# A top-2 mixture-of-experts layer in a two-layer decoder: from all eight experts for every token to 15 gathered blocks of 128 rows per group

## The chip, the cores and the metric

The kernel runs on one core of a Trainium2 chip. The metric is the device time of one execution in microseconds (us), the median over runs. The engines are called as the profile calls them: PE (TensorE matmul) and PEld (its weight load), DVE (VectorE), ACT (ScalarE), POOL (GpSimd) and SP (SyncE, which here only issues DMAs).

## The reference

Activations are `(128, 64, 128)` float32: 128 sequences of 64 tokens, 128 features. Six blocks follow one another, each a residual addition on a layer norm; only the last one changes.

```python
def _L1_ffn_ref(x, gate_W, W1, b1, W2, b2):      # E = 8 experts, 128 -> 256 -> 128, TOP_K = 2
    x_flat = x.reshape(-1, d_in)
    gates = jax.nn.softmax(x_flat @ gate_W, axis=-1)
    tk_g, tk_i = jax.lax.top_k(gates, TOP_K)
    tk_g = tk_g / (jnp.sum(tk_g, axis=-1, keepdims=True) + 1e-08)
    cw = jnp.sum(jax.nn.one_hot(tk_i, E, dtype=x.dtype) * tk_g[..., None], axis=1)
    out = x_flat
    for e in range(E):
        h = jax.nn.relu(x_flat @ W1[e] + b1[e])
        out = out + cw[:, e:e + 1] * (h @ W2[e] + b2[e])
    return out.reshape(x.shape[:-1] + (d_out,))

x = x + _L0_attn_ref(_layernorm(x), ...)     # Mamba-2 block with an MLP
x = x + _L0_xattn_ref(_layernorm(x), ...)    # pointer attention
x = x + _L0_ffn_ref(_layernorm(x), ...)      # ternary feed-forward
x = x + _L1_attn_ref(_layernorm(x), ...)     # causal attention, twice
x = x + _L1_xattn_ref(_layernorm(x), ...)    # cross attention
x = x + _L1_ffn_ref(_layernorm(x), ...)      # the experts
```

`cw` holds two non-zero weights per token: six of the eight experts' results are multiplied by zero.

## The kernel before

**Groups and layers.** The 8192 tokens are cut into 16 groups of 512 (`GT`), each eight sequences, held as four chunks (`C`) of 128 rows. `way(g)` (L1593) takes one group through the ten entries of `LAYERS` (L189), from "prepare" to "experts". A group's activations stay in one of seven SBUF buffers called x (`BUFS`, L186); L1596 loads it and L1603 stores it, and the next group may be loaded into the buffer when the store has landed. Each layer is a token of its own: one group at a time is in it, and up to seven groups are on their way together.

**The order of the work.** It is not written out by hand. `Turns` (L85) is a planner that runs while the program is built. Each piece of work is a generator; `yield V, 0.3` asks for 0.3 us of an engine (V, A, G, T stand for DVE, ACT, POOL, PE), `yield "a"` asks for a buffer of that name (PSUM bank "a": four, "fT": six transposed tiles, "hid": two), `yield None, 2.5` lets time pass for a DMA, and a list starts pieces side by side. The planner serves the process that holds a PSUM bank first, else the oldest request. The order in which it calls the instructions is the fixed order of each engine's queue; DMAs go to SP's queue as they are called. An engine then runs its queue strictly in order, so an instruction that waits holds back all that stands behind it.

**The layer at the end of each group** is `group(g)` in `experts` (L1460 to L1582):

- `norming` (L314): mean and variance on DVE (L283, L284), the root on POOL (L276, L277), the centring on POOL (L312, four instructions per group), then `turning` (L299): four transposes on PE (L305) and one copy by ACT (L307) give `uT`, features by tokens. POOL adds u to the residual (L1471).
- `gating` (L1476): four small matmuls give the logits; a softmax and two rounds of max, compare and rank on DVE leave `cw` (L1519), 128 x 4 x 8. Four transposes of `cw` (L1527), a copy (L1531), four matmuls with the bias table `b2` (L1537) and an addition (L1540) bring in the experts' second bias.
- `expert(e)` (L1552), eight times: `hidden` (L1543) multiplies a 128 x 128 half of `w1` with all 512 tokens (L1547, recorded as L200, the helper `mm`) and ACT takes the relu (L1549); eight matmuls of 128 columns with the halves of `w2` (L1561) leave the result in a bank, and DVE multiplies it by `cw` and adds it to X, a chunk at a time (L1571).

All eight experts' weights lie in SBUF from the start: `w1`, `w2`, `b2` are loaded at L1450 to L1452 (by `load`, L267, so the DMA is recorded at L269).

Of the kernel before, what the change touches and what calls it, by code (L numbers as in the profile page):

```python
# [26 lines left out]
I32 = mybir.dt.int32  # L27
# [12 lines left out]
E = 8  # L40
EXP_LN = "natural_log_exp_and_others"
# [5 lines left out]
def _constants():  # L47
# [26 lines left out]
    put("iota", np.broadcast_to(np.arange(S), (P, S)))  # L74
# [98 lines left out]
def tile_decoder(ctx: ExitStack, tc: tile.TileContext, w: dict, const: bass.AP, out: bass.AP):  # L173
# [12 lines left out]
    BUFS = {"u": 2, "fT": 6, "qm": 3, "km": 4, "x": 7, "hid": 2, "stats": 7, "pT": 12, "inv": 2, "sel": 1, "r2": 2, "r2T": 2, "ctxT": 2, "xdt": 1}  # L186


    LAYERS = ("prepare", "project", "recur", "mlp", "pointers", "ternary", "first", "second", "cross", "experts")  # L189
# [109 lines left out]
    def turning(o, parts, by=ident):  # L299

        yield "a"
        pt = bank("a", by.dtype)
        yield T, 0.12 * len(parts)
        for c, part in enumerate(parts):
            T.transpose(pt[:, c * P : (c + 1) * P], part, by)  # L305
        yield A, ac(P * len(parts))
        A.copy(o, pt)  # L307
        turns.give("a")
# [407 lines left out]
    def pointers(mp):  # L716
# [56 lines left out]
        def group(g):  # L773
# [49 lines left out]
            def ones():  # L823
                for n in range(3):
# [3 lines left out]
                        k["iota"].unsqueeze(1).to_broadcast([P, C, S]),  # L828
# [619 lines left out]
    def experts(mp):  # L1448
        gw = load("gate_W", [P, E], w["L1_ffn_gate_W"], mp)
        w1 = load("moe_w1", [P, E, 256], w["L1_ffn_W1"].rearrange("e d h -> d e h"), mp)  # L1450
        w2 = load("moe_w2", [P, E, 2, P], w["L1_ffn_W2"].rearrange("e (b p) d -> p e b d", p=P), mp)
        b2 = load("moe_b2", [E, P], w["L1_ffn_b2"], mp)  # L1452
# [7 lines left out]
        def group(g):  # L1460
# [3 lines left out]
            u = us[0]  # L1464
            yield "fT"
            uT = wk([P, GT], "fT", bufs=BUFS["fT"])
            yield from turning(uT, [u[:, c, :] for c in range(C)])

# [5 lines left out]
            cw = sm([P, C, E], "cw")  # L1474

            def gating():  # L1476
                yield "a"
                pl = bank("a")
                yield T, 0.9
                for c in range(C):  # L1480
                    mm(pl[:, c * E : (c + 1) * E], uT[:, c * P : (c + 1) * P], gw)
                lg = pl[:, : C * E].rearrange("p (c e) -> p c e", e=E)
                gates = sm([P, C, E], "gates")
                m = sm([P, 3, C], "gm")
                yield V, 0.3
                V.tensor_reduce(m[:, 0], lg, AX.X, ALU.max)
                V.tensor_tensor(gates, lg, over(m[:, 0]), ALU.subtract)  # L1487
                turns.give("a")
                yield A, 0.2
                A.activation(gates, gates, AF.Exp)  # L1490
                yield V, 1.2
                V.tensor_reduce(m[:, 0], gates, AX.X, ALU.add)
                V.reciprocal(m[:, 0], m[:, 0])
                V.tensor_tensor(gates, gates, over(m[:, 0]), ALU.mult)

                one = sm([P, 2, C, E], "one")
                top = sm([P, C], "top")
                for n in range(2):
                    V.tensor_reduce(m[:, n], gates, AX.X, ALU.max)
                    V.tensor_tensor(one[:, n], gates, over(m[:, n]), ALU.is_equal)  # L1500
                    V.tensor_tensor(one[:, n], one[:, n], k["rank"].unsqueeze(1).to_broadcast([P, C, E]), ALU.mult)
                    V.tensor_reduce(top, one[:, n], AX.X, ALU.max)
                    V.tensor_tensor(one[:, n], one[:, n], over(top), ALU.is_equal)
                    if n == 0:
                        V.scalar_tensor_tensor(
                            gates.rearrange("p c e -> p (c e)"),
                            one[:, 0].rearrange("p c e -> p (c e)"),
                            -2.0,
                            gates.rearrange("p c e -> p (c e)"),
                            ALU.mult,  # L1510
                            ALU.add,
                        )
                        yield V, 1.6
                V.scalar_tensor_tensor(m[:, 2], m[:, 0], 1e-8, m[:, 1], ALU.add, ALU.add)
                V.reciprocal(m[:, 2], m[:, 2])
                for n in range(2):
                    V.tensor_tensor(m[:, n], m[:, n], m[:, 2], ALU.mult)
                    V.tensor_tensor(one[:, n], one[:, n], over(m[:, n]), ALU.mult)
                V.tensor_tensor(cw, one[:, 0], one[:, 1], ALU.add)  # L1519

            yield [added(), gating()]

            yield "a"
            pt = bank("a")
            yield T, 0.48
            for c in range(C):
                T.transpose(pt[:E, c * P : (c + 1) * P], cw[:, c, :], ident)  # L1527
            yield "hid"
            cT = wk([P, 2, GT], "hid", bufs=BUFS["hid"])[:E, 0, :]
            yield V, dv(512)  # L1530
            V.tensor_copy(cT, pt[:E, :])  # L1531
            turns.give("a")
            yield "a"
            pb = bank("a")
            yield T, 1.0
# [109 lines left out]
```

## Time and profile before

| What | us |
|---|---|
| median of 3 runs | 2240.68 (2238.79 to 2242.68) |
| the profiled execution, device time | 2244.18 |
| its span, first to last instruction | 2242.4 |
| PE busy | 1943.9 (87%) |
| PEld busy | 1371.6 (61%) |
| DVE busy | 1473.1 (66%) |
| ACT busy | 1159.9 (52%) |
| POOL busy | 1018.7 (45%) |
| mean granted PE clock | 0.918 |
| DMA traffic | 53.61 MB, 24 GB/s on average |

The span is the part of the device time that the profile covers. An engine is busy while an instruction of it runs; instructions that only issue a DMA, wait, or load a register are not counted. A matmul of float32 is recorded as two instructions, so 256 matmuls stand as x512. "busy" of a group counts overlapped instructions once, "mean" is the length of one; for a pipelined engine the first, divided by the count, is what one costs in a stream.

### The profile page before, as it was taken

To read this page: it belongs to the slowest core of one execution; us is meant where nothing else is said; L and a number is where in the kernel's file an instruction comes from. 1 tells how busy PE (TensorE), PEld (TensorE's weight loads), DVE (VectorE), ACT (ScalarE), POOL (GpSimd) and SP (SyncE) were. 2 spreads that over 40 slices of the span, in tenths; PEclk is the share of its full clock that TensorE was granted. 3 is DMA by queue.
4 is the path that set the end of the run, shared out by engine and by line. 5 is a ranking of instruction groups with operands and counts; after the bars stand their busy time and mean duration, and the time that the engine had idled before them with its cause. 6 is when DMAs were issued, how large, how long until landed. Compare 5 with 4: busy or idle time off the path is not lost.

```text
span 2242.4 us, 56838 instructions
## 1 busy us (share of the span) xinstructions
PE 1943.9 (87%) x23919; PEld 1371.6 (61%) x23920; DVE 1473.1 (66%) x3991; ACT 1159.9 (52%) x2133; POOL 1018.7 (45%) x1258
## 2 busy tenths in 40 slices
PE   3777789889998899988998988999889898989996
PEld 1455556566675576666666566666666666756764
DVE  4578786777668567676776775767658567464443
ACT  1445455556465564655554555555537456554542
POOL 2566755554265426372645463435254526151121
PEclk8587788999998998999998989999989999999988
DMA  5111010000010000100101001000001001000000
GB/s 162 39 36 31 27 37 2 23 16 12 26 32 25 20 6 11 34 18 30 31 12 34 14 29 33 13 11 23 20 11 44 9 6 30 2 15 7 11 1 10
DMA packets 73451, 53.61 MB, mean 24 GB/s; under 512 B 30086, under 2 KB 59756, under 8 KB 73196
## 3 DMA queue, kind: packets, MB, share of 16 engines
q1 hardware_dynamic: 73196, 49.99, 7.4%
q8 instruction: 188, 3.08, 0.6%
q14 instruction: 67, 0.55, 0.1%
HBM read 41.45 MB, written 8.52 MB: 22 GB/s over the span
## 4 chain that ended last, share of the span: by engine, by line
PE 52%; DVE 27%; POOL 8%; ACT 8%; issue 3%; DMA 2%; SPq 1%; POOLq 0%; DVEq 0%; ACTq 0%
PE psa L200 36%; PE pss L200 11%; POOL u L312 4%; PE psa L305 4%; DVE tops L1202 3%; DVE x L1571 2%; DVE pT L1145 1%; DVE st L283 1%; DVE mv L284 1%; DVE amx L1157 1%; DVE pT L521 1%; DVE sel L855 1%; DVE s L861 1%; DVE h L1011 1%; DMA x<-in_x 1%
## 5 line engine op out<-in xcount | busy, mean ns | idle before, releaser
L312 POOL TENSOR_SCALAR u<-x,mv,rstd 128x128 f32<-128x128 f32 x320 | 259.6, 823 | 24.2 <-PE psa L305 13.4
L200 PE MATMUL psa<-fT,moe_w 128*128 128x512 f32 x512 | 257.8, 628 | 10.1 <-DVE pT L563 3.3
L200 PEld LDWEIGHTS psa<-moe_w,hid 128*128 128x128 f32 x2048 | 239.9, 192 | 27.6 <-issue 16.2
L1549 ACT ACTIVATE hid<-psa,vcol 128x512 f32<-128x512 f32 x256 | 174.6, 689 | 154.1 <-PE psa L200 151.1
L200 PE MATMUL psa<-moe_w,hid 128*128 128x128 f32 x2048 | 250.2, 277 | 3.0 <-DVE x L1571 1.4
L1571 DVE SCALAR_TENSOR_TENSOR x<-psa,cw,x 128x128 f32<-128x128 f32 x512 | 143.2, 343 | 154.3 <-PE psa L200 154.1
L276 POOL TENSOR_SCALAR rsq<-mv 128x4 f32<-128x4 f32 x96 | 23.4, 244 | 455.4 <-DVE mv L284 391.4
L1235 ACT ACTIVATE pT<-pss 128x512 f32<-128x512 f32 x256 | 146.2, 604 | 132.2 <-PE pss L200 131.9
L1159 POOL TENSOR_TENSOR pT<-pT,amx 128x512 f32<-128x512 f32 x128 | 132.8, 1061 | 110.2 <-DVE amx L1157 97.0
L1202 DVE TENSOR_REDUCE tops<-pss 128x32 f32<-128x2048 f32 x64 | 146.2, 2285 | 39.5 <-PE pss L200 39.3
L1034 POOL TENSOR_SCALAR r<-h 128x512 bf16<-128x512 f32 x64 | 97.2, 1526 | 126.7 <-DVE h L1032 83.4
L200 PEld LDWEIGHTS psa<-fT,moe_w 128*128 128x128 f32 x512 | 91.0, 197 | 92.4 <-issue 59.2
L200 PEld LDWEIGHTS pss<-km,qm 32*128 32x128 f32 x3072 | 101.8, 199 | 43.4 <-issue 34.0
L305 PE MATMUL psa<-cst,u 128*128 128x128 f32 x448 | 84.8, 306 | 45.9 <-POOL u L312 33.8
L200 PE MATMUL pss<-km,qm 32*128 32x128 f32 x3072 | 120.9, 297 | 0.1
L904 POOL TENSOR_TENSOR sel<-hot,s 128x256 f32<-128x256 f32 x64 | 44.3, 711 | 168.2 <-DVE s L898 138.9
L200 PE MATMUL psa<-pT,cst 128*32 128x256 f32 x1536 | 113.6, 405 | 6.0 <-DVE gates L1487 1.4
L617 POOL TENSOR_TENSOR qm<-qm,km 128x256 f32<-128x256 f32 x64 | 47.3, 740 | 155.3 <-DVE qm L612 153.8
L307 ACT COPY fT<-psa 128x512 f32<-128x512 f32 x112 | 65.5, 589 | 100.7 <-PE psa L305 99.7
L1275 ACT ACTIVATE inv<-psa 128x256 f32<-128x256 f32 x96 | 36.7, 383 | 139.0 <-PE psa L200 138.8
L1279 DVE TENSOR_TENSOR fT<-psa,inv 128x256 f32<-128x256 f32 x96 | 40.3, 420 | 99.9 <-ACT inv L1277 99.5
L305 PEld LDWEIGHTS psa<-cst,u 128*128 128x128 f32 x448 | 56.5, 152 | 73.1 <-POOL u L312 45.1
(284 smaller groups left out, 4698.4 us busy)
## 6 DMA issues: line engine op xcount, KB each, us to landing
pT<-steps SPq DMA_DIRECT2D x64, 256.0 KB, 3.9
x<-in_x SPq DMA_DIRECT2D x16, 256.0 KB
mask<-in_mask_Bx1xSxS_ff SPq DMA_DIRECT2D x32, 128.0 KB, 2.8
u<-in_ctx SPq DMA_DIRECT2D x16, 256.0 KB, 2.8
contexts<-ctxT SPq DMA_DIRECT2D x16, 256.0 KB, 2.0
ctxT<-contexts SPq DMA_DIRECT2D x16, 256.0 KB, 3.2
out<-x SPq DMA_DIRECT2D x16, 256.0 KB, 2.3
idg<-in_itok_BxS SPq DMA_DIRECT2D x32, 64.0 KB, 2.9
```

What stands on the lines that cost most here:

```text
L200: T.matmul(o, lhsT=lhsT, rhs=rhs, start=start, stop=stop)
L305: T.transpose(pt[:, c * P : (c + 1) * P], part, by)
L307: A.copy(o, pt)
L312: G.tensor_scalar(u[:, c, :], X[:, c, :], mean(c), scale[:, c : c + 1], ALU.subtract, ALU.mult)
L617: G.tensor_tensor(xc[:, :, cols], xc[:, :, cols], zs[:, :, cols], ALU.mult)
L904: engine.tensor_tensor(part[:, :, i, :], hot[:, n], s3[:, n, i, :].unsqueeze(2).to_broadcast([P, C, S]), ALU.mult,)
L1034: G.tensor_scalar(r2, h[:, c, :], -MAGIC, None, ALU.add)
L1159: G.tensor_tensor(s3, s3, mx.unsqueeze(2).to_broadcast([P, 8, S]), ALU.subtract)
L1202: V.tensor_reduce(mx[:, :, 0:8], banks.rearrange("p r (n s) -> p r n s", s=S), AX.X, ALU.max)
L1235: A.activation(pTs[r].rearrange("p b g q -> p (b g q)"), banks[:, r, :], AF.Exp)
L1549: A.activation(hid[:, b, :], ph, AF.Relu, bias=vec["moe_b1"][:, 2 * e + b : 2 * e + b + 1])
L1571: V.scalar_tensor_tensor(X[:, c, :], po_[:, c * P : (c + 1) * P], cw[:, c, e : e + 1], X[:, c, :], ALU.mult, ALU.add,)
```

## The change

Each token is sent to its two experts only. Per group the 1024 pairs (token, expert) are sorted by expert, each expert's list is padded to whole blocks of 128 rows, and there are at most (1024 + 8 x 127) // 128 = 15 blocks (`BLOCKS`), which are all computed.

- **Layers.** "experts" becomes three: "routing", "experts", "combine". The number of x buffers stays seven. New buffers: xg 2 (gathered rows of four blocks), we 3 (one block's weights), hg 2, yg 2.
- **Routing** (`routed`, `gating`, `routing`): norm and transpose as before; the 512 normed rows are also stored to DRAM (`urows`, two of them, used in turn). `gating` ends at the two one-hot rows and the two weights. `routing` finds each pair's place: two matmuls count the pairs before a row, DVE works out each expert's first block, and eight matmuls against one-hot tiles (`lanes`, 128 x 1024, and `tags`, 128 x 120) turn "which row goes to place p" into `of`, a list of row numbers by place. `to` holds the places by token, `expert` the expert of each block.
- **Experts** (`group`, `four`, `block`): POOL gathers the rows of a block from `urows` with an indirect DMA, one per block; four blocks are transposed together. SP reads the block's expert number from SBUF into a register and loads that expert's weights and both biases, 128 x 642 float32, from `packed`, a DRAM copy made at the start. Two matmuls of 128 columns, two relus by ACT, two matmuls, and a DVE addition of the bias finish a block, and each four blocks are stored to DRAM (`yrows`, two, used in turn).
- **Combine** (`combine`): POOL gathers each token's two result rows, two indirect DMAs per chunk, and DVE multiplies and adds them to X.

Removed are `cw`'s transposes and the bias matmuls, `hidden`, `expert`, and the SBUF copies of the weights. In `turning` the copy covers only the parts transposed.

```diff
+BLOCKS = (2 * GT + E * (P - 1)) // P
-    put("iota", np.broadcast_to(np.arange(S), (P, S)))
+    put("iota", np.broadcast_to(np.arange(P), (P, P)))
+    put("token", np.arange(C) * P + p[:, None])
+    put("before", p[:, None] < p[None, :])
...
-        A.copy(o, pt)
+        A.copy(o, pt[:, : P * len(parts)])
...
-        w1 = load("moe_w1", [P, E, 256], w["L1_ffn_W1"].rearrange("e d h -> d e h"), mp)
-        w2 = load("moe_w2", [P, E, 2, P], w["L1_ffn_W2"].rearrange("e (b p) d -> p e b d", p=P), mp)
-        b2 = load("moe_b2", [E, P], w["L1_ffn_b2"], mp)
+        WIDE = 256 + 2 * P + 2 + P
+        packed = dram.tile([E * P, WIDE], F32, tag="packed", name="packed")
...
+        urows = [dram.tile([GT, P], F32, tag=f"urows{i}", name=f"urows{i}") for i in range(2)]
+        yrows = [dram.tile([BLOCKS * P, P], F32, tag=f"yrows{i}", name=f"yrows{i}") for i in range(2)]
...
+        def whole(x):
+            V.tensor_scalar(x, x, MAGIC, None, ALU.add)
+            V.tensor_scalar(x, x, -MAGIC, None, ALU.add)
...
+        def routing(one, to, of, expert):
+            both = sm([P, C, E], "both", 1)
+            V.tensor_tensor(both, one[:, 0], one[:, 1], ALU.add)
...
+            yield T, 0.4
+            mm(pr[:, 0 : C * E], k["before"], bf)
+            mm(pr[:, C * E : 2 * C * E], k["ones"], bf)
...
+            V.memset(cum[:, 0], 0.0)
+            for c in range(C):
+                V.tensor_tensor(cum[:, c + 1], cum[:, c], total[:, c], ALU.add)
+            V.tensor_scalar(nb[:, 0], cum[:, C], (P - 1) / 2.0, 1.0 / P, ALU.add, ALU.mult)
+            whole(nb[:, 0])
+            V.tensor_tensor_scan(nb[:, 1], k["ones"][:, 0:E], nb[:, 0], 0.0, ALU.mult, ALU.add)
...
+            for n in range(2):
+                V.tensor_tensor(one[:, n], one[:, n], row, ALU.mult)
+                V.tensor_reduce(at[:, :, n], one[:, n], AX.X, ALU.add)
+            V.tensor_copy(to, at)
...
+            V.tensor_copy(expert, which)
+            yield "hid"
+            lanes = wk([P, 2, GT], "hid", bufs=BUFS["hid"]).rearrange("p n (l m) -> p (n l) m", m=P)
...
+            for i in range(2 * C):
+                mm(pi[:, 0:BLOCKS], lanes[:, i, :], tags[:, i, :], i == 0, i == 2 * C - 1)
...
+            V.tensor_copy(of, pi[:, 0:BLOCKS])
+        def routed(g):
             yield from norming(X, us)
+            rows, results = urows[g % 2], yrows[g % 2]
+            nc.sync.dma_start(rows.rearrange("(c p) d -> p c d", p=P), u)
             yield from turning(uT, [u[:, c, :] for c in range(C)])
...
+            yield [added(), gating(g, uT, one, m)]
+            turns.give("fT")
+            yield from routing(one, to, of, expert)
+        def group(g):
+            def four(first):
+                n = min(4, BLOCKS - first)
+                yield "xg"
+                xg = wk([P, 4, P], "xg", bufs=BUFS["xg"])
+                for i in range(n):
+                    yield G, 1.2
+                    G.indirect_dma_start(
+                        xg[:, i, :], None, rows, bass.IndirectOffsetOnAxis(of[:, first + i : first + i + 1], 0)
+                    )
+                yield None, 2.5
...
+                yield from turning(xT[:, 0 : n * P], [xg[:, i, :] for i in range(n)])
+                yield [block(first + i, xT[:, i * P : (i + 1) * P], xg[:, i, :]) for i in range(n)]
...
+                nc.sync.dma_start(
+                    results[first * P : (first + n) * P, :].rearrange("(i p) d -> p i d", p=P), xg[:, 0:n, :]
+                )
+            def block(i, xT, y):
+                yield "we"
+                we = wk([P, WIDE], "we", bufs=BUFS["we"])
+                e = nc.values_load(
+                    expert[0:1, i : i + 1],
+                    engines=[nc.sync.engine],
...
+                nc.sync.dma_start(we, packed[bass.ds(e * P, P), :])
+                yield None, 3.5
...
+                for b in range(2):
+                    mm(ph[:, b * P : (b + 1) * P], we[:, b * P : (b + 1) * P], xT)
...
+                    A.activation(
+                        hg[:, b, :], ph[:, b * P : (b + 1) * P], AF.Relu, bias=we[:, 2 * 256 + b : 2 * 256 + b + 1]
+                    )
...
+                for b in range(2):
+                    mm(py[:, 0:P], hg[:, b, :], we[:, 256 + b * P : 256 + (b + 1) * P], b == 0, b == 1)
...
+                V.tensor_tensor(y, py[:, 0:P], we[:, 514:WIDE], ALU.add)
+            yield [four(first) for first in range(0, BLOCKS, 4)]
+        def combine(g):
+            def chunk(c):
+                yield "yg"
...
+                for n in range(2):
+                    yield G, 1.2
+                    G.indirect_dma_start(
+                        yg[:, n, :], None, results, bass.IndirectOffsetOnAxis(to[:, c, n : n + 1], 0)
+                    )
+                yield None, 2.5
+                for n in range(2):
...
+                    V.scalar_tensor_tensor(
+                        X[:, c, :], yg[:, n, :], m[:, n, c : c + 1], X[:, c, :], ALU.mult, ALU.add
+                    )
+            yield None, 2.5
+            yield [chunk(c) for c in range(C)]
+        stages["routing"], stages["experts"], stages["combine"] = routed, group, combine
```

## The prediction

> **What bounds it now.** First the page's busy times and its 40 slices, then the stretches of the steady part, then SP's DMAs in order of time.
>
> ```profile
> PE 1943.9 (87%) x23919; PEld 1371.6 (61%) x23920; DVE 1473.1 (66%) x3991; ACT 1159.9 (52%) x2133; POOL 1018.7 (45%) x1258
> ...
> PEclk8587788999998998999998989999989999999988
> ...
> PE 52%; DVE 27%; POOL 8%; ACT 8%; issue 3%; DMA 2%; SPq 1%; POOLq 0%; DVEq 0%; ACTq 0%
> ```
> ```profile
> 600.00:900.00 300.00, 272.65 (x3879) 194.78 (x3879) 205.53 (x551) 164.02 (x310) 142.41 (x179) 0.94 0.06 18
> ...
> sum 1500.00, PE 1345.79 PEld 954.33 DVE 1034.53 ACT 823.17 POOL 725.95; mean PE 269.16 PEld 190.87 DVE 206.91 ACT 164.63 POOL 145.19
> ```
> ```profile
> 658.85 0.40 SPq L1603 DMA_DIRECT2D out<-x  x1
> 661.17 0.39 SPq L1596 DMA_DIRECT2D x<-in_x  x1
> ...
> 1628.19 0.39 SPq L1603 DMA_DIRECT2D out<-x  x1
> 1630.52 0.38 SPq L1596 DMA_DIRECT2D x<-in_x  x1
> ```
>
> From 300 to 1800 us PE is busy for 1345.8 of 1500 us (90%), DVE 69%, POOL 48%: PE is the bound there. But the time is also a chain of three stays in an x buffer. Every later x load stands 2.3 us behind a store. The second group enters at the start and leaves at 659; the ninth takes its buffer and leaves at 1628; the sixteenth takes that one and ends the span at 2242. **So what lengthens one group's way is paid three times, what is taken from PE comes back only as far as PE is on that chain.** Of the chain that ended last PE holds 52% x 2242 = 1166 us, 60% of its busy 1944; DVE 605 of 1473, 41%; POOL 179 of 1019, 18%.
>
> **PE, per group.**
>
> ```profile
> L200 PE MATMUL psa<-fT,moe_w 128*128 128x512 f32 x512 | 257.8, 628 | 10.1 <-DVE pT L563 3.3
> L200 PE MATMUL psa<-moe_w,hid 128*128 128x128 f32 x2048 | 250.2, 277 | 3.0 <-DVE x L1571 1.4
> ```
>
> Removed: (257.8 + 250.2) / 16 = 31.75 us, bias matmuls 20.7 / 16 = 1.3, `cw`'s transposes 10.7 / 16 = 0.7: 33.7. Added: 15 blocks of four matmuls, two records each, at 250.2 / 2048 = 0.122 us (the same shape): 14.65; 15 transposes at 71.3 / 512 = 0.14 (the row pT of L305): 2.1; the ten routing matmuls, 20 records at the same 0.122: 2.4. Sum 19.2, so **-14.5 us per group**, -232 in all.
>
> A rule speaks against this step. The Trainium skill, "TensorE: Matmul & The Clock Gate", Back-to-back issue gap, gives a sustained 81 ns for 128 columns and 131 ns for 512: a narrow matmul costs 62% of a wide one. By it the 30 narrow hidden matmuls would cost 18.5 wide ones where 16 stood, 2.5 us more per group. The rows say 0.122 against 0.503 us, 24%: 7.3 us for 16.1. I take the rows, which are this kernel's float32. By the rule the step would save 14.5 - 8.8 - 2.5 = 3.2 us per group, and the sum below would end 88 us later.
>
> **DVE, per group.** Removed: 32 x 143.2 / 512 = 8.95, L1531 and L1540 0.68 each, four small ones of `gating`: 11.1. Added: 15 bias additions and 8 combining ones at 0.28: 6.4; routing: 31 small ones at 0.19 to 0.22 (the last group's gating runs one each 0.22 us), `lanes` of 1024 columns about 1.25 (L826: 458 ns for 256), `tags` and `past` 0.3 each: 8. So **+3.4 us**.
>
> **ACT, per group.** Out 174.6 / 16 = 10.9; in 30 relus of 128 columns at 0.31 (row junk<-u, same width) and four copies at 0.59: 11.6. Nothing, since ACT is half idle.
>
> **POOL, per group: 15 + 8 indirect DMAs.** No row shows one. Below stands SP's issue of a DMA, 0.39; above, the 2.9 us in which the 64 KB load idg<-in_itok lands, if POOL were held all that time. Nearest is POOL's own fixed-cost instruction, L277, 1.04 us for 128 x 4. I take 1.2: 27.6 us on top of 1018.7 / 16 = 63.7, **91 us per group**, beside PE's 121.5 - 14.5 = 107 and DVE's 95. POOL is no bound by that, but no longer free: behind a gather in its queue stand the centrings (L312), whose transposes PE waits for, and the roots (L276) before them. The gathers also bring waits: one for a free xg buffer, that is for the store of earlier blocks to land, and combine's first for the last `yrows` store. If these come late, all of that stands still, for every group under way.
>
> The second rule that speaks against it: the Trainium skill, "SBUF — State Buffer", SBUF: two separate sides, on the "DVE blocks DMA" trap: a descriptor generation on GpSimd is shut out while DVE runs a two-port operation; 620 ns became 3100.
>
> ```profile
> L312 POOL TENSOR_SCALAR u<-x,mv,rstd x320: 782/792/2907, 133.9 to 2194.0; 128x128 f32<-128x128 f32 x160
> ```
>
> Here POOL's centring has a median of 792, a mean of 823 and a worst of 2907 ns: such waits occur, and cost 4% on average. By the row a gather is 1.25 us, by the rule up to 1.2 + 2.5 = 3.7, and POOL 149 us per group. I take the row; the rule widens the top of the range.
>
> **DMA and SP.** 240 weight loads of 321 KB (79 MB), 368 gathers of 64 KB (24 MB): some 75 GB/s on average where the first slice shows 162, so bandwidth is not the limit. A weight load is taken at 4.3 us (pT<-steps, 256 KB, lands in 3.9). The register load before it is not in the trace: between an event's 0.017 and 2.9 us; it waits for nothing but `expert`, so it runs while the load ahead waits for its buffer, and costs the path nothing; at 2.9 SP would hold 43 us more per group, and steps, masks and x loads behind it would be late. Behind a weight load that waits for its buffer stand those same DMAs; the planner calls it when the buffer is given back, so I cost it nothing, and take the 3.3 us per block that a late one could bring (2.9 and an issue) as part of the range. `packed` is written once, in the first 100 us, and first read after 479, where the first group reaches L1471: nothing.
>
> **The longer way of one group,** from the last group, which is nearly alone. Its rounds of compare end at 2201.7, its last addition (L1571) at 2238.9. Changed: three more operations of gating 0.7, routing's DVE work 8.7, 20 matmul records at 0.235 (gating's 8 took 1.88 there, at a granted clock of 0.50) 4.7, hops 0.6: list ready at 2216.4. Four gathers 4.8, landing 2.4, transposes and copy 1.3: 2225. A weight buffer is held for 4.3 + 0.47 + 0.62 + 0.47 + 0.34 and four hops of 0.2 = 7 us; three of them give a block each 2.33 us, 15 blocks 35 us: 2260. Store 2.7, eight gathers 9.6, landing and two additions 3: 2275. **+36 us**, three times: +108.
>
> **Sum.** The other 13 groups on the chain's way: PE -14.5 x 13 x 60% = -113; POOL +27.6 x 13 x 18% = +65; DVE +3.4 x 13 x 41% = +18. With +108: **+78 us** on the profiled execution's 2244.2 (span 2242.4), so 2322; the median of the runs is 3.5 us below that: **2319 us**. One gain is in none of these terms: in before a group holds the last layer alone, from L1471 at 1081.7 to its store at 1182.0, and the next begins at 1195.1, so that layer is occupied almost without a break; in three stages two groups overlap. Worth between nothing (PE is full anyway) and the idle tenth of PE, 150 us over the steady part. I take nothing and leave it to the first rival.
>
> **Rivals.**
> 1. *PE's relief comes back whole* (faster). For it: PE at 90%, a ninth less work, and a last layer that is now split. Against: POOL, DVE and PE come within 16 us of each other, in strictly ordered queues, with still seven groups. If the longer way counts only at the end: -232 + 36 = -196, 2045; with PE's fill over the span falling from 87 to 82% it is 1712 / 0.82 = **2090**. It decides where a gather holds POOL for about 1 us or less.
> 2. *POOL becomes the bound.* A gather at 2.9 us makes 63.7 + 66.7 = 130 us per group, above PE's 107: in my sum +39.1 x 13 x 18% = +92, and on the three ways 3 x 23 x 1.7 = +117: **2525**. Against: the mean of L312.
> 3. *Cancels*: within 5 us of before, where way and relief are equal.
>
> That it does not do what it says is excluded: 15 blocks are computed whatever the routing.
>
> **Numbers.** 0.50 for 2319 (2245 to 2420), 0.29 for the first rival, 0.18 for the second, 0.03 for the third (0.2% is what a measurement can tell). Faster 0.29, same 0.03, slower 0.68. The range 2120 to 2500 leaves out the lower part of rival 1 and the upper of rival 2. With slower cases at 0.68, the likeliest's own range stands above.
>
> **What would show it.** PE's busy time near 1712 us (step 1); a gather's hold on POOL and POOL's waits for it; DVE near 1520; from the last compare to the last addition of the last group 73 us instead of 37; x loads still behind stores, with stays of over 967 us in the middle. Wrong if PE stays near 90% in the middle (rival 1), or if POOL's queue is full (rival 2).

## The result and the profile after

The changed kernel takes **2526.3 us**, median of 4 runs (2513.42 to 2537.8), against 2240.8 beside it (2238.79 to 2242.68): a ratio of 1.1266 (95% interval 1.1232 to 1.1301), 286 us slower. The forecast had the direction; its size, 78 us, was far too small, and 2526 lies beyond its range.

The page after, busy times and granted clock by slices:

```profile
PE 1918.6 (76%) x23648; PEld 1424.2 (56%) x23648; DVE 1566.9 (62%) x4279; ACT 1166.9 (46%) x2421; POOL 1381.7 (55%) x1626
...
PEclk8677899999979888999697899989788988896655
```

PE was to fall by 232 us and fell by 25. The mean granted clock went from 0.918 to 0.851: PE is idle more often, and the last slices stand at 5 to 6. POOL rose by 363, about the 367 that its 368 gathers are busy. The same stretches as before (columns: stretch, its length, then busy us and count for PE, PEld, DVE, ACT, POOL, then clock, DMA share, GB/s):

```profile
600.00:900.00 300.00, 250.02 (x3581) 187.06 (x3582) 195.00 (x530) 151.21 (x320) 167.78 (x194) 0.90 0.28 73
...
sum 1500.00, PE 1212.64 PEld 901.18 DVE 1010.78 ACT 761.00 POOL 869.78; mean PE 242.53 PEld 180.24 DVE 202.16 ACT 152.20 POOL 173.96
```

From 300 to 1800 us PE is now busy 81% of the time (before 90%), DVE 67%, POOL 58%. No engine is full, so something waits. SP's DMAs show where the groups leave:

```profile
848.44 0.40 SPq L1739 DMA_DIRECT2D out<-x  x1
...
850.81 0.38 SPq L1732 DMA_DIRECT2D x<-in_x  x1
...
1796.53 0.39 SPq L1739 DMA_DIRECT2D out<-x  x1
...
1798.90 0.40 SPq L1732 DMA_DIRECT2D x<-in_x  x1
...
2525.49 0.38 SPq L1739 DMA_DIRECT2D out<-x  x1
```

The chain of three stays is still there, but it did not lengthen evenly: the second group leaves 190 us later than before (848 against 659), the stay in the middle takes 946 us instead of 967, and the last one 727 instead of 608. The first group alone is 132 us late: it stores its rows for the gathers at 480, when before it entered the last layer at 479, and leaves at 691 instead of 559.

POOL's longest wait in total is for the store of earlier blocks out of the buffer that a gather fills (total us, times, longest):

```profile
POOL xg L1643 <- DMA yrows<-xg: 162.5, 19, 23.1
```

What a group does in between is shown for the ninth one. First POOL in order of time (start, length; in brackets the idle time before and what ended it), then PE:

```profile
1616.16 1.12 POOL L1643 DMA_INDIRECT xg<-urows,of  x1 [0.18 <-issue]
1623.69 0.94 POOL L1643 DMA_INDIRECT xg<-urows,of  x1 [6.42 <-DMA yrows<-xg]
...
1626.36 1.03 POOL L1705 DMA_INDIRECT yg<-yrows,to  x1 [0.17 <-issue]
1627.69 0.94 POOL L1705 DMA_INDIRECT yg<-yrows,to  x1 [0.30 <-issue]
1628.94 0.94 POOL L1643 DMA_INDIRECT xg<-urows,of  x1 [0.30 <-issue]
...
1636.49 3.25 POOL L316 TENSOR_SCALAR u<-x,mv,r 128x128 f32<-128x128 f32 x4
1639.90 1.03 POOL L1643 DMA_INDIRECT xg<-urows,of  x1 [0.17 <-issue]
1640.98 3.12 POOL L316 TENSOR_SCALAR u<-x,mv,rstd 128x128 f32<-128x128 f32 x4
...
1654.53 0.99 POOL L1643 DMA_INDIRECT xg<-urows,of  x1 [0.16 <-issue]
```
```profile
1651.96 0.66 PE L309 MATMUL psa<-cst,xg 128*128 128x128 f32 x4 [1.25 <-DMA xg<-urows,of]
1657.04 0.48 PE L309 MATMUL psa<-cst,xg 128*128 128x128 f32 x1 [4.42 <-DMA xg<-urows,of]
1657.31 3.06 PE L204 MATMUL psa<-fT,we 128*128 128x128 f32 x12
```

A gather holds POOL for 0.94 to 1.12 us, with 0.30 between two: the 1.2 of the forecast. But the eight that the two xg buffers can take spread from 1616.2 to 1655.5, 39 us. The second stands 6.42 us for the store out of the buffer's last tenant; the others come behind the combining gathers of the group ahead and the centrings and additions of other groups. Only at 1657 does PE meet the first of these blocks, having waited 4.42 us for the last row. The group ahead stored its last block at 1620.9, so for some 36 us no block is computed; from 1697 to 1720, 23 us, no block is computed either: the gathers of the second pair of fours spread from 1685 to 1711. One group at a time is in this layer, and the next group's first gather comes within 14 us, before or behind, of its last store, from the second group to the last: the layer is never empty, and yet in this stay of 135 us (1616 to 1751) it computes no block for 59.

### The profile page after: what moved, and what is told of

The parts are those of the page before. It is cut to its first block, busy times and chain, and to the rows that moved or that the text cites. A ratio compares the mean times of both kernels' runs of the same rounds, so it can differ in the third digit from the quotient of the medians.

```text
span 2529.0 us, 59384 instructions
## 1 busy us (share of the span) xinstructions
PE 1918.6 (76%) x23648; PEld 1424.2 (56%) x23648; DVE 1566.9 (62%) x4279; ACT 1166.9 (46%) x2421; POOL 1381.7 (55%) x1626
## 5 line engine op out<-in xcount | busy, mean ns | idle before, releaser
L1643 POOL DMA_INDIRECT xg<-urows,of x240 | 239.2, 997 | 366.0 <-DMA yrows<-xg 162.5
L1678 ACT ACTIVATE hg<-psa,we 128x128 f32<-128x128 f32 x480 | 156.1, 369 | 220.4 <-PE psa L204 187.4
L204 PE MATMUL psa<-fT,we 128*128 128x128 f32 x960 | 182.3, 335 | 71.6 <-DMA we<-packed 53.4
L311 ACT COPY fT<-psa 128x512 f32<-128x512 f32 (+1 forms) x176 | 101.4, 579 | 262.0 <-PE psa L309 249.6
L204 PEld LDWEIGHTS psa<-fT,we 128*128 128x128 f32 x960 | 153.8, 234 | 101.5 <-issue 39.3
L1689 DVE TENSOR_TENSOR xg<-psa,we 128x128 f32<-128x128 f32 x240 | 67.7, 287 | 205.7 <-PE psa L204 204.8
L204 PE MATMUL psa<-we,hg 128*128 128x128 f32 x960 | 173.8, 318 | 23.5 <-ACT hg L1678 5.3
L204 PEld LDWEIGHTS psa<-we,hg 128*128 128x128 f32 x960 | 145.3, 220 | 43.9 <-ACT hg L1678 12.2
L1705 POOL DMA_INDIRECT yg<-yrows,to x128 | 128.0, 1000 | 56.6 <-issue 28.2
L204 PE MATMUL psa<-pT,v_a 128*32 128x64 f32 x4096 | 87.8, 227 | 13.0 <-issue 12.6
```

What stands on the lines that cost most here:

```text
L204: T.matmul(o, lhsT=lhsT, rhs=rhs, start=start, stop=stop)
L311: A.copy(o, pt[:, : P * len(parts)])
L1643: G.indirect_dma_start(xg[:, i, :], None, rows, bass.IndirectOffsetOnAxis(of[:, first + i : first + i + 1], 0))
L1678: A.activation(hg[:, b, :], ph[:, b * P : (b + 1) * P], AF.Relu, bias=we[:, 2 * 256 + b : 2 * 256 + b + 1])
L1689: V.tensor_tensor(y, py[:, 0:P], we[:, 514:WIDE], ALU.add)
L1705: G.indirect_dma_start(yg[:, n, :], None, results, bass.IndirectOffsetOnAxis(to[:, c, n : n + 1], 0))
```

## Experiments

All times are medians against the kernel before on the same chip (2238 to 2241 us); e1 to e4 ran on chip 0, e5 to e8 on 13, e9 to e12 on 15, e13 to e16 on 3, e17 and e18 on 11. The theories' names (SP, POOL, LENGTH, STAGE, X and so on) are those of the expectations. "Stage pitch" is the time from the first group's last store of blocks to the last group's, divided by 15, read in SP's order: 124.1 us in the changed kernel; the kernel before has 112.0 from output to output.

**Kernels e1 to e4: loads, buffer, price, width.**

```diff
 e1                                           e2
-  e = nc.values_load(expert[0:1, i:i+1])     -  V.tensor_tensor(y, py[:, 0:P], ...)   # y = xg
-  nc.sync.dma_start(we, packed[e])           +  V.tensor_tensor(xT, py[:, 0:P], ...)  # xg given back
+  we = held   # expert 0, loaded once                                                 # after turning
 e3                                           e4 (kernel before)
+  yield None, 2.5                            -  mm(ph, w1[...], uT)
   turns.give("xg")                           +  four mm of 128 columns each
```

e2 and e3 also leave out the 2.5 us that the planner lets pass before `combine`; e2 lets them pass before the transposed rows are given back.

> Leaves out the choice of a block's weights: every block computes with expert 0's, loaded once, so the 240 register loads and 240 weight loads of SP are gone. The order of the instructions on every engine is that of the changed kernel. Theory SP (weight loads that wait for one of three buffers hold up SP's queue, and with it steps, masks, contexts, stores and x loads): most of the 286 us is won back, 2330 us or less, and PE no longer waits for a weight tile (53 us after). Theory POOL (gathers that wait for the store from their xg buffer hold up the roots and centrings behind them): at most 50 us are won, 2475 or more, and POOL's waits for the store of blocks stay near 160 us. Theory LENGTH (simply more steps in series for a group): between the two, since a block loses 4 us of landing but keeps all else; about 2450.

> A block's result is written over its slice of the transposed rows and stored from there, so an xg buffer is free once it is transposed, and no gather waits for a store. Theory POOL: the 162 us in which POOL stood before gathers are gone and 100 to 200 us are won, 2330 to 2430. Theory SP: POOL's waits fall, but the time stays within 40 us, 2485 to 2565. Theory LENGTH: the same, within 40 us.

> Only the planner's times change: the buffer of gathered rows counts as free 2.5 us after the store was issued instead of at once; instructions, buffers and what they wait for are those of the changed kernel, their order is new. Theory that the planner's missing price makes the POOL waits: POOL's waits before gathers fall from 162 us to under 60, and 60 to 150 us are won. Theories SP and LENGTH: within 40 us of 2526. If POOL's waits stay, it is drift between the planned and the real times, not this price.

> The kernel before, with each 512-column product of the hidden layer issued as four of 128 columns. It measures the width price that the prediction took from the rows. By the rows (0.122 against 0.503 us a record): PE's busy time and the time stay within 20 us of before, 2241. By the ratio of the rule that the prediction set aside (a narrow one costs 62% of a wide one): 32 wide products per group of 0.503 become 128 of 0.31, 24 us per group more, 380 us of PE, and some 230 us of time, 2470. Theory PE (blocks cost 0.19 us a record because they are narrow): the new records cost 0.19 us, PE's busy rises by 16 x 32 x 2 x 4 x 0.19 - 258 = 520 us or so.

Measured: e1 **2450.5** (ratio 1.0978, 1.0937 to 1.1018; pitch 118.9), e2 **2535.1** (1.1340, 1.1313 to 1.1366), e3 **2587.4** (1.1553, 1.1516 to 1.159), e4 **2242.6** (1.0017, 1.0005 to 1.003).

e1 falsifies theory SP in its strong form: with all 240 weight loads gone, 76 of the 286 us come back, and the time is the 2450 that LENGTH named. In the changed kernel SP stands 760 us before weight loads whose buffer is not free (total us, times, longest):

```profile
SPq L1667 <- DVE xg L1689: 760.3, 136, 48.6
```

So about a tenth of that wait is paid in time. e2 moved POOL's wait and did not remove it, and its time, 9 us longer, is where SP and LENGTH had it. POOL's waits in e2:

```profile
POOL yg L1707 <- DMA yrows<-fT: 238.5, 11, 41.3
POOL rsq L280 <- DVE mv L288: 189.4, 31, 27.6
```

No gather of rows waits for a store any more, but now combine's first gather of a group stands up to 41 us for the last blocks. POOL takes its instructions in the planned order; whichever of them depends on blocks that are behind plan stops it. e3 shows two things: the price alone did not cure the waits (135.7 us before gathers of rows, 100.6 before those of combine), and a new order with no instruction changed is worth +61 us here, more than any theory allowed. e4 settles the width: by the rule that the forecast set aside it would be some 230 us slower, and it is 3. The row of the hidden layer's products in 128 columns (busy us, mean ns):

```profile
L200 PE MATMUL psa<-fT,moe_w 128*128 128x128 f32 x2048 | 263.7, 283 | 10.3 <-DVE pT L563 3.3 <-ACT qm L1076 2.8 <-ACT hid L1550 1.4
```

263.7 us for four times the instructions of before's 257.8: 0.129 us a record. In this kernel's float32 a narrow product costs about what its columns cost (0.129 against 0.503). The products of the changed kernel's blocks cost more:

```profile
L204 PE MATMUL psa<-fT,we 128*128 128x128 f32 x960 | 182.3, 335 | 71.6 <-DMA we<-packed 53.4 <-DVE m L894 4.2 <-ACT hg L1678 2.5
L204 PE MATMUL psa<-we,hg 128*128 128x128 f32 x960 | 173.8, 318 | 23.5 <-ACT hg L1678 5.3 <-ACT r2T L311 3.3 <-issue 2.2
```

That is 0.19 and 0.18 us a record. They come four records at a time, 0.61 to 0.71 us a burst at the higher clock and 1.2 at the lower. Width is excluded by e4; that short bursts and the lower clock make the difference is what the rows suggest, not something that a run isolated.

**Kernels e5 to e8: the single stay.**

```diff
 e5: layer "experts" has two tokens instead of one, three pairs of DRAM tables
 e6:
-    for i in range(n):
-        yield G, 1.2
+    yield G, 1.2 * n
+    for i in range(n):
         G.indirect_dma_start(xg[:, i, :], None, rows, ...)
 e7: e2 and e6, and  turns.give("fT", 2.5)   # free 2.5 us later, the group is not held back
 e8: e7 and e5
```

> The planner lets two groups be in the experts layer at once (with three pairs of row tables in DRAM instead of two); buffers, instructions and everything else are those of the changed kernel. Theory STAGE: one group at a time is in the stage of gathers and blocks, it stays there 128 us on average, the next begins within some 5 us, so the time is 509 (first gather) + 16 x 128 + 18; by it, overlap of the stays must shorten the time, here by 3 to 10 us per group because both groups still share two xg buffers and three weight buffers: 2370 to 2480. Theory LENGTH (steps in series for one group, paid three times through the seven x buffers): nothing is taken from a group's way, within 30 us of 2526. Theory that PE or POOL is full: within 30 us too, or slower.

> POOL's gathers of four blocks are asked of the planner as one turn of 4.8 us instead of four turns of 1.2, each behind whatever POOL has been asked meanwhile. In the changed kernel the 8 gathers of two such turns spread over 39 us in one group (1616 to 1655) where they take 10 us of POOL, and no block computes meanwhile. Theory STAGE: a stay loses 10 to 20 us, 160 to 300 us in all, 2230 to 2370. Theory POOL (what stands behind the gathers is what is late): centrings and roots are later by up to 3.6 us each turn, no gain or slower, 2500 to 2600. Theory LENGTH: 10 to 20 us three times, 30 to 60 us, 2470 to 2500.

> One group at a time as in the changed kernel; results written over the transposed rows (an xg buffer is free once it is transposed), the planner counts a row buffer as free 2.5 us after the store was issued without holding the group back, and the gathers are asked for in one turn. Theory STAGE: the second pair of gathers no longer waits for the first pair's blocks, so a stay loses the second empty stretch (35 us in the group looked at) and some of the first: 25 to 45 us, and the time falls by 300 or more, 2000 to 2230 unless another bound takes over near 2150. Theory LENGTH: 25 to 45 us three times, 2390 to 2450. Theory POOL: as in the run with results over the rows alone, near 2530.

> All of the run before it, and two groups in the experts layer at once. Theory STAGE: the stay is no bound any more, the time is that of the engines: POOL 88 us and PE some 110 us per group, 2050 to 2200, faster than the kernel before. Theory LENGTH: no better than with one group, within 30 us of that run.

Measured: e5 **2441.7** (1.0898, 1.0871 to 1.0924; pitch 118.1), e6 **2487.1** (1.1110, 1.1067 to 1.1152; pitch 121.9), e7 **2410.5** (1.0753, 1.0722 to 1.0784), e8 **2408.7** (1.0739, 1.0702 to 1.0777; pitch 116.7). Letting two groups in wins 85 us with no SBUF buffer and no instruction changed, within the range that STAGE named. The other sizes that STAGE named were too large (e6 wins 39 of 160 to 300, e7 116 of 300 or more), and e6, e7 and e8 came out where LENGTH had them. In e7 the layer stands empty for up to 107 us ahead of a group, in e8 for up to 63, and their times hardly differ. So the single stay may have been one bound, of some 85 to 118 us, with another close beneath it. That is not shown: each of the four is also a new order.

**Kernels e9 to e12: x buffers, and loads again.** e9 is e1, e10 the kernel before, each with `"x": 8` (e10 makes room by one buffer instead of two for the small tiles `gates` and `one`); e11 is e8 with `"x": 8, "xg": 1`; e12 is e8 with e1's edit.

> The kernel of e1 (every block computes with expert 0's weights, held in SBUF; no register and weight loads, otherwise as changed) with eight x buffers instead of seven; the room is that of the two weight buffers that e1 no longer has. Against e1's 2450.5. Theory LENGTH, which is the prediction's (a chain of three stays in an x buffer): with eight buffers the sixteenth group has one group before it in its buffer instead of two, so one stay of the three goes, and 100 us or more are won, 2350 or less. Theory STAGE (the experts layer holds one group at a time and is never empty): an eighth group only waits longer before that layer, 2420 to 2480.

> The kernel before with eight x buffers (the room is made by one buffer each instead of two for the two small tiles gates and one). Before, the last layer is empty for 87 us ahead of the eighth group, which waits for the first group's x buffer, and for 55, 51 and 17 elsewhere. Theory X (that gap is the wait for the buffer): 40 to 90 us are won, 2150 to 2200. Theory that PE is full at 90%: within 25 us of 2240.

> The kernel of e8 (two groups in the experts layer, results over the transposed rows, gathers in one turn) with eight x buffers; the room is made by one buffer of gathered rows instead of two, which can only slow a stay. In e8 the stage stands empty for 63 us ahead of the eighth group and 20 to 60 us ahead of others, so it is no bound there. Theory X (with the stage relieved the x buffers bind again): 60 to 150 us are won against e8's 2409, 2260 to 2350. Theory ENGINES (PE at 82% and POOL at 60% in strict orders is all that can be had): within 40 us of 2409.

> The kernel of e8 without the register and weight loads (every block computes with expert 0's weights, held in SBUF). SP still stands 700 us in e8 before weight loads whose buffer isn't free, with the steps, masks and x loads behind them. Theory SP: once the stage is relieved these waits are what binds, 100 to 200 us are won, 2210 to 2310. Theory ENGINES or X: as in e1, the landings alone, 30 to 80 us, 2330 to 2380.

Measured: e9 **2417.2** (1.0770, 1.0735 to 1.0806), e10 **2252.4** (1.0045, 1.0031 to 1.0059), e11 **2349.0** (1.0469, 1.0446 to 1.0492; pitch 110.8), e12 **2325.7** (1.0368, 1.0342 to 1.0394; pitch 111.5). With an eighth buffer the kernel *before* is 12 us slower, where theory X named 40 to 90 us won. The order is new there and two small tiles lost a buffer, so this is weak evidence, but it gives no sign that the x buffers bind. The chain of three stays through seven buffers stays true as a description of who waits for whom. In e9 the eighth buffer wins 33 us, where LENGTH named 100 or more. e11 wins 60 against e8, the least that theory X named. The loads are worth 83 us in e12, much as in e1 and less than SP named.

**Kernels e13 and e17: the gathers themselves.**

```diff
 e13 = e1 and                                       e17 = e13 and, before each of these loads,
-  G.indirect_dma_start(xg[:, i, :], ...)           +  G.tensor_scalar(fill, fill, 1.0, None, ALU.mult)
+  nc.sync.dma_start(xg[:, i, :], rows[i*P:(i+1)*P])
   (the same for yg)
```

> The kernel of e1 without the sorting: instead of POOL's 23 gathers per group SP loads 64 KB of rows in their plain order (and every block computes with expert 0's weights); the order of everything else on PE, VectorE, ScalarE and POOL is that of the changed kernel. Against e1's 2450.5. Theory POOL GATHERS (the 39 us in which a stay waits for gathers spread over POOL's queue): the stay falls from 124 us to under 105, and the time by 150 to 300 us, 2150 to 2300. Theory ORDER (the planner's order on PE and POOL, which is unchanged, keeps the blocks where they are): within 60 us of e1, 2390 to 2450.

> The kernel of e13 (no gathers on POOL, plain loads by SP, expert 0's weights for every block) with an operation of 128 x 160 elements on a tile of its own, about 1 us, in the place of each of POOL's 368 gathers: POOL is as busy as with them, but these wait for nothing, and rows don't come through POOL. Against e13's 2245 and e1's 2450.5. Theory TIME (POOL's occupied time is the cost): 2390 to 2450. Theory WAITS (what the gathers wait for and hold up, and that rows come only at POOL's turn): 2245 to 2310.

Measured: e13 **2245.0** (1.0018, 1.0008 to 1.0028; pitch 106.4), e17 **2265.9** (1.0118, 1.0078 to 1.0159; pitch 107.8). With the order of all other work as in the changed kernel, 205 us go with the gathers; loads and gathers together are 281 of the 286. On the page of e13 POOL is back at its busy time of before, and the chain that ended last is mostly PE and DVE, as before:

```profile
PE 1804.3 (80%) x23647; PEld 1354.4 (60%) x23648; DVE 1522.5 (68%) x4279; ACT 1161.9 (52%) x2421; POOL 1019.8 (45%) x1258
...
PE 43%; DVE 31%; ACT 11%; POOL 6%; DMA 4%; issue 4%; SPq 1%; ACTq 0%; POOLq 0%; DVEq 0%
```

e17 gives POOL an occupation back in the gathers' places. It came out shorter than meant, 0.61 us instead of 1:

```profile
L1646 POOL TENSOR_SCALAR fill<-fill x240: 597/609/1554, 506.4 to 2211.2; 128x160 f32<-128x160 f32 x120
L1700 POOL TENSOR_SCALAR fill<-fill x128: 598/608/1177, 641.8 to 2216.7; 128x160 f32<-128x160 f32 x128
```

POOL's busy time rises by 226 us to 1246, and the time by 21. Scaled to the gathers' 367 busy and their pauses of 0.30 (368 x 0.30 = 110), POOL's time would cost 21 x 477 / 226 = 44 us. That is an estimate: e17 gives back less than half of the time, and no run fills all of it. The other 160 are what the gathers do beyond holding POOL, first of all waits: rows that come only at POOL's turn, gathers that stand for a store, and roots and centrings behind them. PE's waits show a part of it (total us, times, longest), in e1, in e13 and in e17:

```profile
PE psa L309 <- POOL u L316: 44.5, 40, 11.5
PE psa L309 <- DMA xg<-urows,of: 41.7, 22, 4.7
```
```profile
PE psa L309 <- POOL u L316: 19.3, 25, 4.3
...
PE psa L309 <- DMA xg<-urows: 5.4, 8, 1.6
```
```profile
PE psa L309 <- POOL u L316: 21.5, 23, 6.8
```

The 42 us for rows fall to 5 in e13, and those for centrings more than halve; with POOL busier by 226 us in e17 the latter stay low. The profiled span of e13 is 199 us shorter than that of e1. PE's idle gaps are 112 of them: 62 in these two rows, 32 in gaps of e1 that end at no wait the profile shows (the next part returns to them), the rest in small ones. PE's busy time is another 76; at a granted clock of 0.900 instead of 0.869 it would fall by 64 (1880 x 0.869 / 0.900 = 1815), an estimate. A limit of this pair: SP's plain loads also need no list, so e13 takes the wait for the list away as well, and which of the waits weighs most is left open.

**Kernels e14 to e16 and e18.** e14 is e12 with plain loads. e15 is e12 with `"x": 9`. e16 is e11 with the rows stored by POOL and the weight loads in ScalarE's queue. e18 is e11 with the centrings of `norming` on VectorE.

> The kernel of e12 (two groups in the layer, results over the rows, gathers in one turn, no weight loads) with plain loads by SP in place of POOL's 23 gathers per group. Against e12's 2325.7. Theory POOL (its 367 us of gathers, in order before roots and centrings, are what is left): 100 to 200 us are won, 2130 to 2230, below before. Theory PE and LENGTH: PE's relief is 107 us of busy time and not the 232 of the sum, at most 40 us are won, 2285 to 2340.

> The kernel of e12 with nine x buffers instead of seven. Against e12's 2325.7. Theory X: two more groups in flight fill the gaps of 80, 75 and 69 us ahead of the eighth to tenth group, 80 to 160 us are won, 2165 to 2245. Theory ENGINES: within 40 us of 2326.

> A complete kernel: that of e11 (two groups in the layer, results over the rows, gathers in one turn, eight x buffers), the rows stored to DRAM by POOL, which makes them, and the register and weight loads given to ScalarE's queue as planned turns of 0.6 us, so that SP holds no load that waits for a weight buffer. Against e11's 2349. Theory SP: 40 to 100 us are won, 2250 to 2310. Theory ORDER: ScalarE's queue now waits for the weight buffers and holds up relus, copies and exponentials, slower than e11 by 20 to 100 us.

> A complete kernel: that of e11 with the centrings of norming (256 of 320, 0.81 us each on POOL) given to VectorE at about 0.2 us each, so that POOL does 13 us per group less and PE no longer waits behind gathers for a centring. Against e11's 2349. Theory POOL (what stands behind the gathers in its queue is late): 60 to 150 us are won, 2200 to 2290, about before's time. Theory that the blocks' own way is what is left: within 30 us, 2320 to 2380.

Measured: e14 **2194.5** (0.9776, 0.974 to 0.9813; pitch 104.4), e15 **2444.4** (1.0906, 1.0875 to 1.0937), e16 **2436.8** (1.0875, 1.0821 to 1.093), e18 **2437.2** (1.0883, 1.0837 to 1.093). e14 repeats the gathers' cost in another order: 131 us. The other three lost: e15 119 us against e12, e16 and e18 88 each against e11. Only for e16 had a theory, ORDER, named a loss (20 to 100). In e15, with nine groups started at once, the first is 60 us later at its last store (693 against 632), and the pitch is 115.2. One possible reason is that the planner makes a new order each time, and by e3 an order alone can be worth 61 us.

The traces show a second one. PE and POOL at the same moment, in e11:

```profile
690.03 1.12 PE L204 MATMUL psa<-pT,v_x 128*32 128x64 f32 x64
```
```profile
690.07 0.94 POOL L1706 DMA_INDIRECT yg<-yrows,to  x1 [0.30 <-issue]
```

The same in e18:

```profile
693.81 0.32 PE L204 MATMUL psa<-pT,v_x 128*32 128x64 f32 x4 [1.10 <-issue]
694.54 0.27 PE L204 MATMUL psa<-pT,v_x 128*32 128x64 f32 x1 [0.40 <-issue]
695.26 0.43 PE L204 MATMUL psa<-pT,v_x 128*32 128x64 f32 x3 [0.46 <-issue]
```
```profile
692.96 0.95 POOL L1643 DMA_INDIRECT xg<-urows,of  x1 [0.30 <-issue]
694.21 0.94 POOL L1643 DMA_INDIRECT xg<-urows,of  x1 [0.30 <-issue]
695.45 0.94 POOL L1643 DMA_INDIRECT xg<-urows,of  x1 [0.30 <-issue]
```

In e11 a stream of 64 records runs through beside a gather. In e18 PE gets a few records out every 0.7 us while POOL gathers, and its gaps end at no wait that the profile shows ("issue"). All such gaps of PE, in us:

| Run | Gaps | Mean of 64 records beside or just behind a gather |
|---|---|---|
| changed kernel; e1, e2, e3 | 27; 32, 68, 37 | 2.7; 2.2, 3.6, 3.2 |
| e5 to e8, e9, e11, e12 | 0 to 10 | 1.2 |
| e15, e16, e18 | 128, 86, 80 | 5.1, 4.7, 4.2 |
| the kernels without gathers | 0 to 1.5 | none |

Away from gathers such a stream takes 1.1 to 1.2 us on average in every run. So beside gathers PE's own stream slows in some runs and not in others. The runs that have gathers and few gaps are exactly those on chips 13 and 15 (the chip of the changed kernel's run is not on record), but no kernel with gathers ran on two chips, so whether the chip, the order or something else decides it is open.

This limits what can be read from the times. The 88 us of e16 and e18, the 119 of e15 and the 33 of e9 (32 us of gaps in e1, 3 in e9) are of the size of these gaps and can't be put down to the edits, nor can theory X be called refuted by e15. The 85 of e5 and the 60 of e11 are new orders, and a part of the former can be the changed kernel's 27 us of gaps. No complete kernel tried beats the one before; the best is e11. e14, which leaves out sorting and the choice of weights, is 46 us faster than before; whether another order of it would win more was not tested.

## Why the forecast was wrong

**What bounds the kernel.** "What lengthens one group's way is paid three times" failed: the loss is 190 us up to the second group's end, -21 in the middle stay, 119 in the last, not three equal parts. An eighth x buffer wins nothing before (e10). After, a layer that one group holds at a time is never empty; that it binds in place of the buffers is suggested by e5 and not shown, since e13 keeps that layer and is still 281 us faster than the changed kernel.

**PE.** "-14.5 us per group", PE's busy time near 1712: measured 1918.6. The width rule was rightly set aside (e4). The term that was mis-sized is 0.122 us for a record of a block: 0.185 on average, 1920 x 0.063 = 122 us; the transposes took 51.9 instead of 34, 18 more; the other 66 fall to all other products, and go with a clock of 0.851 instead of 0.918. Even in e13, the same order without gathers and weight loads, PE's busy time is 1804.

**POOL.** The size of a gather was right: 1.25 us in a stream. As POOL's time it costs 44 us by the estimate from e17, not 65. The second rule set aside, of a gather shut out by VectorE, hardly shows in this trace: of 368 gathers, mean 1.00 us, five take over 1.3 and the longest 1.93, each beside a VectorE operation with two inputs in SBUF (L922, L525). The rival with gathers of 2.9 us named 2525 (its terms sum to 2528) and is refuted nonetheless: the number is right by accident.

**The waits of the gathers: the step that failed.** The forecast named them: "If these come late, all of that stands still, for every group" — and gave them no price. They came late: 162.5 us of waiting for a store in 19 gathers, and a group's eight gathers spread over 39 us. In the kept order the gathers cost 205 us, where the forecast had 65 for their length alone. By the estimate from e17 about 160 (205 less 44) are what it had put at nothing: these waits, what is late behind them, and PE's streams that slow down beside a gather, of which it did not think. How the 160 divide among the three is open.

**Weight loads.** "The planner calls it when the buffer is given back, so I cost it nothing": measured 76 us (e1; 83 in e12). The register loads themselves, 0.26 to 0.76 us, are within the bounds given. The range had 3.3 us per block for late loads; 76 / 240 is 0.32.

**The longer way.** A group alone was to take 36 us more. The last group takes 143 us from its last compare to its last addition, instead of 73. Block by block the forecast's 7 us for a weight buffer was right where nothing waits: of the last group's 15, nine are held for 6.6 to 7.9 us from the load's issue to the addition, but six for 14 to 29. From the first gather to the last store the group takes 70 us (2440 to 2510), 4.7 a block instead of 2.33; in e13, without gathers and without weight buffers to wait for, the same stretch takes 31 (2205 to 2237). What was missing is that the first group does not travel alone: its way is 132 us longer with six groups around it, and still 116 in e13.

**The sum.** Without its POOL term the forecast reads -113 + 18 + 108 = +13. e13, which has neither gathers on POOL nor weight loads, measures +4, made of +155 in the first two groups (814 against 659) and some -150 later, where PE's relief is. That the sums agree is in part luck: both sides are larger than forecast (+108; -113 + 18), and PE's busy time in e13 fell by 140 us and not 232. What is left of the miss is that the 65 us for POOL should have been 281 for gathers and loads. DVE was forecast near 1520 and is 1567.

## What to carry to other kernels

An instruction that can wait, put into an in-order queue that others share, is to be priced by what stands behind it while it waits, not by its length: here 23 gathers of 1.25 us per group cost some 44 us in all as POOL's time and some 160 by the rest (estimates from e17). Before counting on relief of the fullest engine, ask which layer or buffer admits one tenant at a time, and how long it is held with the other groups running beside it, since a group timed alone at the end shows only the shortest stay. And where a planner makes the order, test an edit once with the order kept: here a new order alone was worth 61 us (e3). When an edit loses for no reason that can be seen, compare one and the same stream of an engine in both traces: here 64 records took 1.1 us in one and over 4 in the other.

## What the runs showed of the hardware

A gather of 128 rows of 512 B holds POOL for 0.96 us (median of the changed kernel's 368), and the next one starts 0.30 later. Its mean is 1.00 us where VectorE is busy all the while and 0.98 where VectorE is idle; the five over 1.3 us stand beside VectorE operations with two inputs in SBUF.

Beside gathers PE's stream of 64 short records took 2.2 to 5.1 us in seven runs and 1.2 in seven others; without a gather beside it, 1.1 to 1.2 in all of them. What decides this is open.

The granted clock went with PE's fill: 0.918 at 87% busy (before), 0.90 at 80% (e13), 0.869 at 77% (e1), 0.851 at 76% (after). So a part of the idle time was paid for again in PE's own busy time, by the estimate above 64 us between e1 and e13.

On POOL an operation with constant scalars took 0.61 us for 128 x 160, while the centring with two operands per partition takes 0.81 on average for 128 x 128.
